# Two-layer cross-attention: where the turn of the row maxima stands in TensorE's order in layer 1

## The chip, the cores and the metric

One Trainium2 chip, of which the kernel uses one core. The metric is device microseconds (us) of one execution. The kernel before has three timed runs; their median is what a later time is held against.

## The reference, cut to what matters

Two layers of cross-attention follow each other, each with its own weights. There are 16 batches, 256 query rows of 320 channels, 20 heads of 16 channels, and 256 context rows of 512 channels, of which the first 252 are text and the last 4 are image tokens in layer 2; layer 1 takes the first 77 as text and the other 179 as image tokens. For layer 1:

```python
text = encoder_hidden_states[:, :77]
ip = encoder_hidden_states[:, 77:]
q = hidden_states @ Wq
probs = softmax(q_h @ k_h.T * scale)                 # per head, 77 text columns
text_probs = softmax(q @ k_text.T * scale)           # once over all channels
sem = (text_probs @ text) @ ip.T * scale
fused = q_h @ ip_k_h.T * scale + 0.5 * sem           # per head, 179 image columns
out = (probs @ v_h + spatial_mask * softmax(fused) @ ip_v_h) @ Wout + bout + hidden_states
```

Layer 2 is of the same kind, with a normalised semantic term. Each softmax subtracts a row maximum before its exp; this document is about where that maximum is brought into place in layer 1.

## The kernel before, in words

**Slots.** The work of layer 1 is cut into 80 slots, one for each batch and group of four heads (five groups a batch, so ten slots are two batches); layer 2 has 80 more. A slot of layer 1 takes some 7.7 us. `slot0(k)` (L783) writes down what TensorE does in slot k: the first half of the scores of slot k+2, the first half of the weights of slot k, attention on the values for slot k-1, the second half of the scores of k+2, the second half of the weights of k, the loads for slot k+4, and in the third quarter the turn of the maxima of k+2. Numbers between these steps (0.2, 0.6, 1.0) are places where `fill` puts in the work of other tasks that is due then: projections (L609, L612 queries with `hq` and outputs with `ho`; L239, L249 products of keys and values with weights `wA` to `wD`), transposes of `sp` (L685), scores for the semantic term (L666).

**The scores and their maxima.** `score0` (L737 on) writes four matmuls (L744) into the one score buffer `S`, which spans two banks. VectorE takes the maxima out of it in two reductions, L745 over the 77 text columns and L746 over the 179 others, into `mn`. Only then may the next half of scores go into `S`. So each slot has two score halves, each followed by its pair of reductions.

**The turn of the maxima.** `maxima0` (L748) is what the change moves. Two small matmuls (L752) with the identity turn `mn` of both halves into rows, in one of three `X` banks. ScalarE casts these rows to `mt` (L754, one buffer), and four DMAs of 2 KB each (L756), issued from ScalarE's own queue, put them into rows of the query stack `qs`. The second L752 needs the maxima of the second half, so it needs the L746 that follows the second L744 of the same slot.

**Who uses them.** `turned0` (L758 on) multiplies the key stack with the query stack, maxima rows included (L768, into two `T` banks); ScalarE takes the exp (L771), GpSimd multiplies by `rs` (L774). The second exp of slot k is ordered behind the last of the DMAs of the maxima of k+1. `attend0` multiplies with the values (L800, 24 matmuls into the single bank `P`), and `settle0` on VectorE transposes it (L811 into `nt`), takes the reciprocal (L814), multiplies (L815) and writes `tmp` (L817); L817 is the last to read bank `P`, so the next L800 waits for it. Every fifth slot the result of a batch is complete: `gather` (L830, transposes into `hT`) and `split` (L282 a cast on ScalarE; L283 and L284 on VectorE, into `ho`) prepare it for the output projection.

**What sets the order.** TensorE's order is what the program says. The order on ScalarE, VectorE, GpSimd and SyncE is set at build time by a scheduler that models a timeline, with a few instructions held in program order. So when TensorE's order changes, instructions on the other engines can change places too.

Of the kernel before, what the change touches and what calls it, by code (L numbers as in the profile page):

```python
# [38 lines left out]
SIZES = dict(RAW=2, KST=2, NP=4, NR=4, CTA=2, CTB=2, WB=4, M=2)  # L39
NS = B * NG  # L40
LEAD = 4


def RAMP(t):
# [6 lines left out]
def xattn2(  # L51
# [685 lines left out]
    def score0(k, t):  # L737
        Q, K = QK[k]
        if t == 0:
            maxes[k] = buf("mn", [128, 2, 4, 2], FR, bufs=2)  # L740
        mn = maxes[k]
        sp = scores(True)
        for h in range(4):
            mm(sp[:, h], Q[: XROW + T0, h, t * 128 : (t + 1) * 128], K[: XROW + T0, h], start=True, stop=True)  # L744
        nc.vector.tensor_reduce(mn[:, t, :, 0], sp[:, :, :T0], axis=AX.X, op=ALU.max)  # L745
        anchor(nc.vector.tensor_reduce(mn[:, t, :, 1], sp[:, :, T0:], axis=AX.X, op=ALU.max))  # L746
# [11 lines left out]
    def turned0(k, t):  # L758

        rs = get("s0", k // NG)[2]  # L760
        Q, K = QK[k]
        for p in range(2):
            if t == 0:
                P[k, p] = buf("P", [128, 2, 2, S], bufs=SIZES["NP"])
        st = [own("T").rearrange("p (h t) -> p h t", h=2) for p in range(2)]
        for p in range(2):
            for j in range(2):
                mm(st[p][:, j], K[:KS0, 2 * p + j, t * 128 : (t + 1) * 128], Q[:KS0, 2 * p + j], start=True, stop=True)  # L768
        for p in range(2):
            pt = P[k, p][:, t]  # L770
            exp = anchor(nc.scalar.activation(pt, st[p], AF.Exp, scale=SCALE))  # L771
            if t and k + 1 in issues:
                queued(exp, issues[k + 1])
            anchor(nc.gpsimd.tensor_mul(pt, pt, rs[:, t : t + 1].to_broadcast([128, 2, S])))  # L774

    def attend0(k):
        b, g = divmod(k, NG)
        v, pv = get("v0", b), own("P")
        for vt in range(3):
            values0(k, pv, v, vt)  # L780
        settle0(b, g, pv)

    def slot0(k):  # L783
        yield lambda: ahead(k + 2, 0)
        yield lambda: turned0(k, 0)
        yield 0.2
        if k > 0:
            yield lambda: attend0(k - 1)
        yield lambda: ahead(k + 2, 1)
        yield lambda: turned0(k, 1)  # L790
        yield lambda: stacks(k + LEAD)
        yield 0.6
        yield lambda: maxima(k + 2)
        yield 1.0

    def values0(k, pv, v, vt):
# [81 lines left out]
    def both1(k, t):  # L878

        a = k + 2 < 2 * NS and QK[k + 2]   # L880
        c = NS <= k < 2 * NS and QK[k]
        if a:
            if t == 0:
                maxes[k + 2] = buf("mn", [128, 4, 4], FR, bufs=2)[:, :2]
            sp = scores()
        def turned():
            for j in range(2):
                for u in range(2):
                    rows = slice(64 * u, 64 * u + KS1)
                    mm(st[u][:, j], c[1][rows, j, lo : lo + 128], c[0][rows, j], start=True, stop=True)  # L890

        def plain():
            for j in range(2):
                for u in range(2):
                    rows = slice(64 * u, 64 * u + XROW)
                    mm(sp[:, 2 * u + j], a[0][rows, j, t * 128 : (t + 1) * 128], a[1][rows, j], start=True, stop=True)  # L896
            image_scores(k + 2, t, sp)
            anchor(nc.vector.tensor_reduce(maxes[k + 2][:, t], sp[:, :, :T1], axis=AX.X, op=ALU.max))  # L898

        if c:  # L900
            st = [bank("T").rearrange("p (h t) -> p h t", h=2) for u in range(2)]
            lo = (0, DUP)[t]
        for wanted, make in ((a, plain), (c, turned))[:: 1 if t == 0 else -1]:
            if wanted:
                make()
        if c:
            for u in range(2):
                if t == 0:
                    P[k, u] = buf("P", [128, 2, 2, S], bufs=SIZES["NP"])
                anchor(nc.scalar.activation(P[k, u][:, t], st[u], AF.Exp, scale=SCALE))  # L910
# [13 lines left out]
    def rounded1(k, u):  # L924
        R[k, u] = buf("ctb", [128, 2, 2, S], FR, bufs=SIZES["CTB"], name="ph")
        W[k, u] = buf("wB", [128, 2, 2, S], bufs=SIZES["WB"], name="wt")
        for t in range(2):
            nc.scalar.activation(R[k, u][:, t], P[k, u][:, t], AF.Copy, scale=0.5)  # L928
            anchor(nc.gpsimd.tensor_sub(W[k, u][:, t], P[k, u][:, t], f(R[k, u][:, t])))  # L929
# [33 lines left out]
    def slot1(k):  # L963
# [12 lines left out]
        if mine:  # L976
            yield lambda: rounded1(k, 0)
        yield lambda: stacks(k + LEAD)
        if last:
# [207 lines left out]
    for c in range(B // 2):  # L1187
        n, k = 10 * c, [("k0", c)] if c else []
# [33 lines left out]
    def stacks(k):  # L1222
        if 0 <= k < 2 * NS:
            (stacks0 if k < NS else stacks1)(k)

    def ahead(k, t):
        if k < NS:
            score0(k, t)
        else:
            both1(k - 2, t)  # L1230

    def maxima(k):
        if k < 2 * NS:
            (maxima0 if k < NS else maxima1)(k)
# [225 lines left out]
```

## Time and profile before

| | |
|---|---|
| runs | 1503.99, 1501.08, 1503.84 us; median 1503.84 |
| profiled execution, its own time | 1502.55 us |
| its span in the trace | 1500.7 us |
| TensorE busy | 1422.2 us, 95% |
| VectorE busy | 1179.7 us, 79% |
| GpSimd busy | 1212.4 us, 81% |
| ScalarE busy | 889.5 us, 59% |
| TensorE's mean granted clock | 0.99 |

The trace covers the span; some 1.85 us of the execution's own time lie around it. Lines of instructions read: start in us, duration in us, engine, line of the kernel, operation, output<-inputs, how many in a row (x), and in brackets how long the engine stood idle before it and what it then waited for. Slots 28 to 38 of layer 1 lie from about 282 to 359 us, and layer 1 ends near 690 us.

### The profile page before, as it was taken

What the parts mean: (1) busy time and instruction counts of PE and PEld (TensorE: products, weight loads), DVE (VectorE), ACT (ScalarE), POOL (GpSimd) and SP (SyncE); (2) the same over time, 40 slices, a digit from 0 to 9 for tenths busy, and PEclk for the clock granted to TensorE, in tenths of its full rate; (3) what the DMA queues carried; (4) which work ended last, traced back from release to release, by engine and by line L of the source; (5) the groups of instructions that cost most, each with busy time, mean ns of one, the idle gap of its engine ahead of it and who ended that gap; (6) DMA issues with size and microseconds to landing.
All of it is one profiled execution on the core that took longest, in us unless ns stands there. A gap on an engine that the chain in (4) does not pass through costs nothing.

```text
span 1500.7 us, 36096 instructions
## 1 busy us (share of the span) xinstructions
PE 1422.2 (95%) x12740; PEld 1148.3 (77%) x12740; DVE 1179.7 (79%) x2593; ACT 889.5 (59%) x1975; POOL 1212.4 (81%) x1304
## 2 busy tenths in 40 slices
PE   8789999999999999789999999999999999999997
PEld 7678788888878877567777777777777777777765
DVE  5467777777778787878887788878877887788786
ACT  5356565656555655456665666566656665666563
POOL 4269797979787887898698779877987798779887
PEclk9799999999999999999999999999999999999999
DMA  7867777868676776774534434443444344433411
GB/s 234 202 200 211 199 221 196 226 190 223 185 207 193 219 217 167 199 214 145 165 99 130 124 116 118 131 128 112 121 131 128 110 122 127 130 109 99 121 30 44
DMA packets 230986, 234.32 MB, mean 156 GB/s; under 512 B 39127, under 2 KB 200678, under 8 KB 230790
## 3 DMA queue, kind: packets, MB, share of 16 engines
q1 hardware_dynamic: 228598, 230.71, 55.1%
q8 instruction: 102, 1.67, 0.5%
q10 hardware_dynamic: 2208, 1.30, 0.4%
q14 instruction: 78, 0.64, 0.1%
HBM read 118.04 MB, written 77.04 MB: 130 GB/s over the span
## 4 chain that ended last, share of the span: by engine, by line
PE 70%; DVE 13%; DMA 6%; POOL 5%; issue 3%; ACT 2%; SPq 1%; ACTq 0%; DVEq 0%; POOLq 0%
PE X L938 15%; PE X L239 14%; PE P L800 6%; PE X L609 5%; PE P L950 5%; PE P L960 4%; PE S L744 3%; PE T L890 3%; PE S L896 3%; DVE mn L746 3%; PE T L768 3%; PE X L612 2%; DVE nt L811 2%; PE X L578 2%; POOL P L774 1%
## 5 line engine op out<-in xcount | busy, mean ns | idle before, releaser
L774 POOL TENSOR_TENSOR P<-P,rs 128x512 f32<-128x512 f32 x320 | 413.7, 1314 | 89.8 <-ACT P L771 88.4
L929 POOL TENSOR_TENSOR wt<-P,ctb 128x512 f32<-128x512 f32 x320 | 410.7, 1307 | 74.0 <-ACT ctb L928 74.0
L938 PE MATMUL X<-ctb,gm 128*128 128x512 f32 x1120 | 305.4, 402 | 5.7 <-DVE wt L939 5.6
L771 ACT ACTIVATE P<-T 128x512 f32<-128x512 f32 x320 | 175.9, 595 | 151.1 <-PE T L768 120.6
L939 DVE TENSOR_TENSOR wt<-X,wt 128x512 f32<-128x512 f32 x320 | 216.5, 681 | 42.2 <-PE X L938 36.0
L938 PEld LDWEIGHTS X<-ctb,gm 128*128 128x128 f32 x1120 | 195.2, 188 | 39.0 <-DVE wt L939 8.6
L910 ACT ACTIVATE P<-T 128x512 f32<-128x512 f32 x320 | 173.2, 593 | 76.1 <-PE T L890 73.1
L928 ACT ACTIVATE ctb<-P 128x512 fp32r<-128x512 f32 x320 | 186.5, 627 | 38.9 <-PE X L938 33.5
L898 DVE TENSOR_REDUCE mn<-S 128x4 fp32r<-128x1008 f32 x160 | 191.5, 1197 | 0.0
L746 DVE TENSOR_REDUCE mn<-S 128x4 fp32r<-128x716 f32 x160 | 142.6, 891 | 0.0
L800 PE MATMUL P<-P,vr 128*32 128x256 f32 x1920 | 125.5, 392 | 7.2 <-DVE tmp L817 4.2
L744 PEld LDWEIGHTS S<-ks,qs 125*128 125x128 f32 x640 | 89.6, 194 | 39.9 <-issue 19.4
L744 PE MATMUL S<-ks,qs 125*128 125x256 f32 x640 | 114.4, 302 | 6.0 <-DMA ks<-M 3.7
L1027 POOL TENSOR_TENSOR r<-u,rs 128x40 f32<-128x40 f32 (+2 forms) x17 | 108.7, 6393 | 4.0 <-DVE u L1024 4.0
L745 DVE TENSOR_REDUCE mn<-S 128x4 fp32r<-128x308 f32 x160 | 74.9, 468 | 42.7 <-PE S L744 41.9
L768 PE MATMUL T<-qs,ks 127*128 127x256 f32 x640 | 105.5, 288 | 0.1
L800 PEld LDWEIGHTS P<-P,vr 128*32 128x32 f32 x1920 | 56.8, 112 | 48.2 <-issue 9.9
L768 PEld LDWEIGHTS T<-qs,ks 127*128 127x128 f32 x640 | 90.1, 194 | 0.9 <-issue 0.3
L950 PE MATMUL P<-P,v1t 128*32 128x256 f32 x1280 | 85.7, 385 | 0.0
L960 PE MATMUL P<-wt,zone 128*32 128x256 f32 x1280 | 84.6, 379 | 0.3 <-DVE wt L939 0.3
L811 DVE STREAM_TRANSPOSE nt<-P 128x512 f32<-128x512 f32 x80 | 57.0, 712 | 34.3 <-PE P L800 33.6
L239 PE MATMUL X<-wC,cta 128*128 128x324 f32 (+1 forms) x474 | 78.4, 312 | 0.0
(297 smaller groups left out, 2974.0 us busy)
## 6 DMA issues: line engine op xcount, KB each, us to landing
qd<-q SPq DMA_DIRECT2D x96, 256.0 KB
qs<-tph SPq DMA_DIRECT2D x64, 320.0 KB
rawc<-in_cT_dram SPq DMA_DIRECT2D x60, 256.0 KB
qs<-qd SPq DMA_DIRECT2D x80, 192.0 KB
ks<-kd SPq DMA_DIRECT2D x80, 192.0 KB
ks<-kd SPq DMA_DIRECT2D x160, 96.0 KB
qs<-qd SPq DMA_DIRECT2D x160, 96.0 KB
kd<-kst SPq DMA_DIRECT2D x57, 256.0 KB
```

What stands on the lines that cost most here:

```text
L239: last = mm(out, lhs(a, k), rhs(b, k), start=i == 0, stop=i == len(terms) - 1)
L744: mm(sp[:, h], Q[: XROW + T0, h, t * 128 : (t + 1) * 128], K[: XROW + T0, h], start=True, stop=True)
L746: anchor(nc.vector.tensor_reduce(mn[:, t, :, 1], sp[:, :, T0:], axis=AX.X, op=ALU.max))
L768: mm(st[p][:, j], K[:KS0, 2 * p + j, t * 128 : (t + 1) * 128], Q[:KS0, 2 * p + j], start=True, stop=True)
L771: exp = anchor(nc.scalar.activation(pt, st[p], AF.Exp, scale=SCALE))
L774: anchor(nc.gpsimd.tensor_mul(pt, pt, rs[:, t : t + 1].to_broadcast([128, 2, S])))
L800: mm(pv[32 * s : 32 * s + 32, o : o + S], v[:, vt, h : h + 32], P[k, s // 2][:, t, s % 2], start=vt < 2, stop=vt != 1,)
L898: anchor(nc.vector.tensor_reduce(maxes[k + 2][:, t], sp[:, :, :T1], axis=AX.X, op=ALU.max))
L928: nc.scalar.activation(R[k, u][:, t], P[k, u][:, t], AF.Copy, scale=0.5)
L929: anchor(nc.gpsimd.tensor_sub(W[k, u][:, t], P[k, u][:, t], f(R[k, u][:, t])))
L938: mm(yp, gm[:, gb], R[k, u][:, kt], start=i == 0, stop=i == len(blocks[n]) - 1)
L939: nc.vector.tensor_mul(W[k, u][:, n], yp, W[k, u][:, n])
```

## The change

The turn of the maxima of slot k+2 stood in the third quarter of slot k. It now stands at the very beginning of slot k+1, in front of that slot's first scores, for the maxima of slots 2 to 58. From slot 57 on the old place is kept, so slot 57 issues two turns, 58 at its start and 59 in its third quarter. Nothing is computed otherwise, and no instruction is added or taken away.

```diff
+SOON = 57
...
     def slot0(k):
+        if 0 < k <= SOON:
+            yield lambda: maxima(k + 1)
         yield lambda: ahead(k + 2, 0)
         yield lambda: turned0(k, 0)
         yield 0.2
...
         yield lambda: turned0(k, 1)
         yield lambda: stacks(k + LEAD)
         yield 0.6
-        yield lambda: maxima(k + 2)
+        if k >= SOON:
+            yield lambda: maxima(k + 2)
         yield 1.0
```

In the changed kernel line numbers are 1 higher up to the slot function and 4 higher behind it (the two L752 become L753, L744 to L746 become L745 to L747, L800 becomes L804, L811 L815, L817 L821, L830 L834; L283 and L284 become L284 and L285).

**TensorE, slot 32.** Before, the turn (L752) stands between two pieces of filling work, the products with `cta` and `ctb` alone and those with `wC`:

```order
L744 MATMUL S<-ks_101,qs_97 128x256 x4
L768 MATMUL T<-qs_95,ks_99 128x256 x4
L239 MATMUL X<-cta_81 77x192 x3
L239 MATMUL X<-cta_82 77x192 x3
L239 MATMUL X<-ctb_83 77x192 x3
L239 MATMUL X<-ctb_84 77x192 x3
L752 MATMUL X<-ident_r,mn_566 8x128 x2
L239 MATMUL X<-wC_92,cta_81 128x320 x3
L239 MATMUL X<-wC_92,cta_82 128x320 x3
L239 MATMUL X<-wC_92,ctb_83 128x320 x3
L239 MATMUL X<-wC_92,ctb_84 128x320 x3
L744 MATMUL S<-ks_102,qs_98 128x256 x4
```

Now the same piece of TensorE's order reads:

```order
L769 MATMUL T<-qs_95,ks_99 128x256 x4
L240 MATMUL X<-cta_81 77x192 x3
L240 MATMUL X<-cta_82 77x192 x3
L240 MATMUL X<-ctb_83 77x192 x3
L240 MATMUL X<-ctb_84 77x192 x3
L240 MATMUL X<-wC_92,cta_81 128x320 x3
L240 MATMUL X<-wC_92,cta_82 128x320 x3
L240 MATMUL X<-wC_92,ctb_83 128x320 x3
L240 MATMUL X<-wC_92,ctb_84 128x320 x3
L753 MATMUL X<-ident_r,mn_566 8x128 x2
L745 MATMUL S<-ks_102,qs_98 128x256 x4
```

The turn has moved behind the twelve `wC` matmuls and stands right in front of the next slot's first scores. On TensorE only these pairs move, 52 of the 80, each past 5 to 29 matmuls; the maxima of slots 10, 20, 30, 40 and 50 have no filling work in between and stay where they were.

**VectorE, slots 31 and 32 (place A in what follows).** The rows are the attention of slot 30 being settled (`nt_136`, `tmp_807`), with the gathering (`hT`) and splitting (`ho`) of a finished batch and the maxima of two slots (`mn_567` and `mn_566`). Before:

```order
L830 STREAM_TRANSPOSE hT_1308<-hsn 128x256
L167 TENSOR_TENSOR q_145<-X,q_145 128x256
L811 STREAM_TRANSPOSE nt_136<-P 128x512
L745 TENSOR_REDUCE mn_567<-S 128x4
L746 TENSOR_REDUCE mn_567<-S 128x4
L814 RECIPROCAL P<-nt_136 128x16
L283 TENSOR_TENSOR ho_161<-hT_1308,ho_161 128x512
L284 SCALAR_TENSOR_TENSOR ho_161<-ho_161,tmask,hT_1308 128x256
L815 TENSOR_TENSOR P<-P,mk 128x8
L260 TENSOR_TENSOR X<-X,kst_160 64x2x179
L817 TENSOR_TENSOR tmp_807<-nt_136,P 128x256
L745 TENSOR_REDUCE mn_566<-S 128x4
```

Now:

```order
L815 STREAM_TRANSPOSE nt_136<-P 128x512
L834 STREAM_TRANSPOSE hT_1300<-hsn 128x256
L746 TENSOR_REDUCE mn_567<-S 128x4
L747 TENSOR_REDUCE mn_567<-S 128x4
L818 RECIPROCAL P<-nt_136 128x16
L284 TENSOR_TENSOR ho_161<-hT_1300,ho_161 128x512
L285 SCALAR_TENSOR_TENSOR ho_161<-ho_161,tmask,hT_1300 128x256
L819 TENSOR_TENSOR P<-P,mk 128x8
L746 TENSOR_REDUCE mn_566<-S 128x4
L747 TENSOR_REDUCE mn_566<-S 128x4
L821 TENSOR_TENSOR tmp_807<-nt_136,P 128x256
L261 TENSOR_TENSOR X<-X,kst_160 64x2x179
```

The `hT` transpose has come to stand behind the attention's transpose, in front of the reductions, and the next pair of reductions has come in front of the multiplication that writes `tmp`. The same holds in slots 12, 22, 42 and 52.

**VectorE, slots 36 and 37 (place B).** Here `nt_135` is the attention of slot 35, `ho` the other batch, and the two pairs of reductions are those of the second half of slot 36 (`mn_566`) and of the first half of slot 37 (`mn_567`). Before:

```order
L830 STREAM_TRANSPOSE hT_1308<-hsn 128x256
L283 TENSOR_TENSOR ho_161<-hT_1308,ho_161 128x512
L284 SCALAR_TENSOR_TENSOR ho_161<-ho_161,tmask,hT_1308 128x256
L811 STREAM_TRANSPOSE nt_135<-P 128x512
L745 TENSOR_REDUCE mn_566<-S 128x4
L746 TENSOR_REDUCE mn_566<-S 128x4
L814 RECIPROCAL P<-nt_135 128x16
L815 TENSOR_TENSOR P<-P,mk 128x8
L817 TENSOR_TENSOR tmp_808<-nt_135,P 128x256
L745 TENSOR_REDUCE mn_567<-S 128x4
L746 TENSOR_REDUCE mn_567<-S 128x4
```

Now:

```order
L815 STREAM_TRANSPOSE nt_135<-P 128x512
L746 TENSOR_REDUCE mn_566<-S 128x4
L747 TENSOR_REDUCE mn_566<-S 128x4
L818 RECIPROCAL P<-nt_135 128x16
L834 STREAM_TRANSPOSE hT_1300<-hsn 128x256
L819 TENSOR_TENSOR P<-P,mk 128x8
L821 TENSOR_TENSOR tmp_808<-nt_135,P 128x256
L284 TENSOR_TENSOR ho_161<-hT_1300,ho_161 128x512
L285 SCALAR_TENSOR_TENSOR ho_161<-ho_161,tmask,hT_1300 128x256
L746 TENSOR_REDUCE mn_567<-S 128x4
L747 TENSOR_REDUCE mn_567<-S 128x4
```

The split into `ho` has moved from in front of the attention's transpose to behind `tmp`, right in front of the first half's reductions of slot 37. On ScalarE its cast (L282, now L283) now stands behind the cast of `rs` and two casts of `rawc` into `cta`, in front of which it stood. The same holds in slots 7, 17, 27, 47 and 57.

Elsewhere, near the end of the moved turns (**place C**, slots 57 to 59), VectorE's multiplication L455 of `rawc`, which needs a load, stands in front of the reductions of the second half of slot 57; before it stood behind them. On ScalarE the cast and the four DMA issues of a turn now stand around the two exps of the first half of a slot, where they were spread over a slot's end and the next one's beginning. GpSimd and SyncE have small moves only, and layer 2 keeps its order but for a few rows at the very end.

## The prediction

> **What bounds the kernel now.** I read the page first, then TensorE's waits and groups, then the timelines of the places where the order changes.
>
> ```profile
> PE 1422.2 (95%) x12740; PEld 1148.3 (77%) x12740; DVE 1179.7 (79%) x2593; ACT 889.5 (59%) x1975; POOL 1212.4 (81%) x1304
> ```
>
> TensorE is busy for 95% of the span, so only what shortens its waits, or adds to them, can move the time. TensorE's row of groups for the turn and its waits, first in slots 1 to 57 (75 to 521 us), then in the ten slots 28 to 37 (282 to 359 us), are:
>
> ```profile
> L752 PE MATMUL X<-ident_r,mn 128*8 128x128 f32 x160 | 30.4, 229 | 25.6 <-DVE mn L746 23.2 <-DVE mx L673 1.8
> ```
>
> ```profile
> PE X L752 <- DVE mn L746: 12.3, 22, 0.8
> PE P L800 <- DVE tmp L817: 2.3, 6, 0.4
> ...
> PE X L752 <- DVE mn L746: 2.3, 4, 0.8
> PE P L800 <- DVE tmp L817: 0.4, 1, 0.4
> ```
>
> The turn's wait for the reduction L746 is the largest wait of layer 1: 12.3 us in 22 places of slots 1 to 57, 2.3 us in every ten slots. The wait for L817 is the second, and it is the one that place A will touch. The 25.6 us of the whole group are not all in reach: 12.3 lie where turns are moved, the rest lie in the first 75 us and in slots 58 on, where nothing moves.
>
> **What goes.** TensorE's timeline, with a turn that doesn't wait, one that waits in full, and one that waits a little:
>
> ```profile
> 304.18 0.28 PE L752 MATMUL X<-ident_r,mn 128*8 128x128 f32 x2
> ...
> 318.65 0.22 PE L752 MATMUL X<-ident_r,mn 128*8 128x128 f32 x1
> 319.49 0.23 PE L752 MATMUL X<-ident_r,mn 128*8 128x128 f32 x1 [0.62 <-DVE mn L746]
> 319.56 1.09 PE L239 MATMUL X<-wC,cta 128*128 128x320 f32 x6
> 320.49 0.75 PE L239 MATMUL X<-wC,ctb 128*128 128x320 f32 x4
> ...
> 350.59 0.58 PE L752 MATMUL X<-ident_r,mn 128*8 128x128 f32 x2
> ```
>
> A pair that doesn't wait takes 0.28 us in all; the pair at 318.65 ends at 319.72, so it takes 1.07, or 0.79 more: the 0.62 of wait and some 0.16 of overlap that it loses. The pair at 350.59 takes 0.58, 0.30 more. So ten slots lose 2.3 + 4 x 0.16 + 0.30 = 3.24 us to the turn. In five times ten slots that is 16.2 us. The first slots have what is left of the 12.3 us, 12.3 - 5 x 2.3 = 0.8, and with two overlaps 1.1 us: **17.3 us in reach**.
>
> Would the wait really go? At the new place some filling work stands in front of the turn. For the turn above it is twelve `wC` matmuls, of which the two rows above cover ten in 1.7 us, against a wait of 0.79. A turn that comes that much later finds L746 done. What is late next is the first half of scores (L744) right behind it, which needs the same reduction to have emptied `S`; it comes after the same filling work, as before. So I take all 17.3 us away, on condition that VectorE does its reductions when it did.
>
> **What comes: place A, five times.** VectorE's and TensorE's timelines, slots 31 and 32:
>
> ```profile
> 308.29 0.43 DVE L830 STREAM_TRANSPOSE hT<-hsn 128x256 f32<-128x256 f32 x1
> 308.65 0.38 DVE L167 TENSOR_TENSOR q<-X,q 128x256 fp32r<-128x256 f32 x1
> 309.28 0.72 DVE L811 STREAM_TRANSPOSE nt<-P 128x512 f32<-128x512 f32 x1 [0.25 <-PE P L800]
> 309.93 0.48 DVE L745 TENSOR_REDUCE mn<-S 128x4 fp32r<-128x308 f32 x1
> 310.32 0.90 DVE L746 TENSOR_REDUCE mn<-S 128x4 fp32r<-128x716 f32 x1
> 311.13 0.25 DVE L814 RECIPROCAL P<-nt 128x16 f32<-128x16 f32 x1
> 311.29 1.39 DVE L283 TENSOR_TENSOR ho<-hT,ho 128x512 fp32r<-128x512 f32 x1
> 312.60 1.52 DVE L284 SCALAR_TENSOR_TENSOR ho<-ho,tmask,hT 128x256 fp32r<-128x256 f32 x1
> 314.11 0.52 DVE L260 TENSOR_TENSOR X<-X,kst 64x358 f32<-64x358 f32 x1
> 314.55 0.40 DVE L817 TENSOR_TENSOR tmp<-nt,P 128x256 f32<-128x256 f32 x1
> ```
>
> ```profile
> 315.10 1.50 PE L800 MATMUL P<-P,vr 128*32 128x256 f32 x24 [0.43 <-DVE tmp L817]
> ```
>
> The attention matmuls already wait here for L817, so every delay of L817 shows in full. L830 (308.29 to the next start at 308.65, 0.36) moves behind L811 into this chain, a pair of reductions (309.93 to 311.22, 1.29) comes in front of L817, and L260 (314.11 to 314.55, 0.44) leaves it: 0.36 + 1.29 - 0.44 = **1.2 us**. The lower bound is given by the other L284 below, which takes 0.47 in place of 1.52: then 0.2. The upper: on ScalarE three DMA issues of the turn now stand in front of the cast that feeds L283,
>
> ```profile
> L756 ACTq DMA_DIRECT2D qs<-mt x312: 569/570/1203, 64.2 to 682.7; - x156
> ```
>
> and one of them at its longest instead of its median adds 0.63: 1.8 us. The median issues end just before VectorE is ready for `ho`, so I take 1.2, five times: 6.0 us.
>
> **Place B, six times.** ScalarE's, VectorE's and TensorE's timelines, slots 36 and 37:
>
> ```profile
> 346.39 0.82 ACT L282 CAST ho<-hT 128x768 fp32r<-128x768 f32 x1
> ...
> 349.82 1.15 ACT L164 CAST cta<-rawc 128x512 fp32r<-128x512 f32 x2
> ```
>
> ```profile
> 347.25 1.45 DVE L283 TENSOR_TENSOR ho<-hT,ho 128x512 fp32r<-128x512 f32 x1 [1.12 <-ACT ho L282]
> 348.62 0.47 DVE L284 SCALAR_TENSOR_TENSOR ho<-ho,tmask,hT 128x256 fp32r<-128x256 f32 x1
> ```
>
> ```profile
> 355.43 0.74 PE L744 MATMUL S<-ks,qs 125*128 125x256 f32 x4
> ```
>
> The cast of `ho` now follows the two `cta` casts, so it runs from 350.97 to 351.79. L283 (1.45) ends at 353.24, L284 at 353.7 to 354.8 (0.47 or 1.52), and the pair of reductions behind them (1.29) at 355.0 to 356.1. TensorE comes for `S` at 355.43: it waits 0 to 0.6 us, up to 1.0 if the cast is held up as well. I take 0.5, six times: 3.0 us.
>
> Which of the two L284 values holds depends on GpSimd:
>
> ```profile
> 309.47 4.37 POOL L774 TENSOR_TENSOR P<-P,rs 128x512 f32<-128x512 f32 x3
> ...
> 348.81 0.23 POOL L434 MEMSET M<- 77x154 f32 x1 [0.67 <-PE X L696]
> ```
>
> The slow L284 (312.60) lies wholly beside a GpSimd multiplication, the fast one (348.62) beside 0.2 us of GpSimd idle and a MEMSET. GpSimd works at both places of the changed kernel unless its multiplications come later, so I took the slow one for A. The Trainium skill, page "GPSIMD Engine Reference", section "1. Specifications", says that GpSimd shares its memory interfaces with VectorE, with contention where a VectorE instruction has two inputs there; these rows agree, and by it A falls to 0.2 wherever GpSimd is idle beside L284, which would make the sum 5 us better.
>
> **Place C, once.** SyncE's, VectorE's and TensorE's timelines, slots 57 to 59:
>
> ```profile
> 518.98 0.52 SPq L84 DMA_DIRECT2D rawc<-in_cip_dram  x1
> ```
>
> ```profile
> 521.53 1.04 DVE L455 TENSOR_TENSOR rawc<-rawc 64x512 f32<-64x512 f32 x1 [0.37 <-DMA rawc<-in_cip_dram]
> ...
> 522.57 1.43 DVE L284 SCALAR_TENSOR_TENSOR hq<-hq,tmask,xq 128x256 fp32r<-128x256 f32 x1
> ```
>
> ```profile
> 521.60 0.29 PE L752 MATMUL X<-ident_r,mn 128*8 128x128 f32 x2
> ...
> 525.13 1.24 PE L800 MATMUL P<-P,vr 128*32 128x256 f32 x17
> ...
> 529.19 0.23 PE L752 MATMUL X<-ident_r,mn 128*8 128x128 f32 x1 [1.22 <-DVE mn L746]
> ```
>
> With L455 in front, the reductions of slot 57 start at 522.57 and end at 523.86, and the turn that ran at 521.60 waits 2.3 us. L817, now behind L284 and another pair of reductions, moves from before 525.13 to about 529, some 1.6 us beyond that. Behind it the turn at 529.19 loses the 1.22 of wait that it had, but runs at about 532.5. Net **3.3 us**; 0 if the load comes with the earlier stream and is there in time, 5 if both stalls add up. Another 0.3 us comes in slot 4, where L817 also gets two instructions in front.
>
> A stall of 2.3 us could also cost clock. Two windows (their length, then the busy time of TensorE, its weight loads, VectorE, ScalarE and GpSimd, then granted clock, share of the DMA engines and GB/s), and TensorE's longest waits from 600 to 650 us:
>
> ```profile
> 515.00:690.00 175.00, 154.72 (x1434) 125.65 (x1432) 142.37 (x315) 94.54 (x222) 146.80 (x164) 0.96 0.71 194
> ...
> 600.00:650.00 50.00, 39.18 (x361) 30.36 (x365) 42.73 (x94) 25.42 (x60) 42.59 (x45) 0.90 0.75 199
> ```
>
> ```profile
> PE X L752 <- DVE mx L673: 1.8, 1, 1.8
> ```
>
> No wait there was over 1.8 us, and yet the granted clock fell to 0.90, a loss of at most 5 us of TensorE's time. The Trainium skill, page "TensorE: Matmul & The Clock Gate", section "HAM oscillation — how this bites in real kernels", has the rule that TensorE should have no idle gap over some 3.4 us; by it C costs no clock. This trace speaks against relying on that. I leave the clock out of the sum and put it into the slower case.
>
> **The sum.** -17.3 + 6.0 + 3.0 + 0.3 + 3.3 = -4.7 us against the profiled execution's own 1502.55 (span 1500.7 and 1.85 around it): 1497.9. The median of the runs, 1503.84, is 1.3 above that execution, so the forecast is **1499.1** as a median. A measurement of this kernel can tell about 0.2%, 3 us, from no change; the forecast is just beyond that.
>
> **The rivals.**
> 1. *The whole gain.* VectorE has room (79% busy), ran ahead in the changed places, and A, B and C cost nothing: 1503.84 - 17.3 = 1486.5. For it: the lower bounds of A, B and C are all near 0. Against it: L800 waits for L817 at place A already. Chance 0.17.
> 2. *The wait only moves.* The first scores behind the turn need the same reduction; where VectorE's pair comes later, TensorE waits at L744 in place of L752, or the lead of layer 1 is given back from 521 us on, where loads set the pace. 1503.8. For it: from 515 to 690 us TensorE is idle for 20 of 175 us, so there is room to lose it. Against it: the filling work in front is longer than the wait. Chance 0.18.
> 3. *Slower: VectorE's queue.* Long instructions (the `ho` pair, L455) stand in front of L817 and the reductions, and TensorE stalls there for longer than the turn did. It decides once 5 A + 6 B + 0.3 + C exceeds 17.3. At the upper bounds 5 x 1.8 + 6 x 1.0 + 0.3 + 5 = 20.3, or +3.0, and with 0 to 5 us of lost clock, 1506.8 to 1511.8; I take 1508.5. For it: every upper bound has a row. Against it: all must come together. Chance 0.20.
>
> **How the numbers follow.** The forecast has a chance of 0.45, with its own range 1494 to 1503, from the bounds of A and B at less than their ends together: a fifth of it, 0.09, lies above 1500.8, within 3 us of no change. Faster: 0.17 + 0.36 = 0.53. Same: 0.18 + 0.09 = 0.27. Slower: 0.20. The range leaves out the lower half of the whole gain and the upper half of the slower case: 1488 to 1508. So faster is likely by a little more than even, and a gain of a few us is the likeliest.
>
> **What would show it.** Right: in slots 1 to 57 the turn's wait for the reduction falls from 12.3 us to under 2; at the end of place A L800's wait for the L817 of before grows from 0.43 to about 1.6, once in ten slots; the second scores at B wait about 0.5 for their reduction; the load of `rawc` is named on VectorE just ahead of the reductions at C. Wrong: the turn, or the scores behind it, still waits for the reduction in every ten slots; new waits for the maxima's DMAs ahead of L768; ten slots of 77 us that shrink by over 2.5 or not at all; or a stretch after 521 us that grows by as much as layer 1 gained.

## The result, and the profile after

The changed kernel takes **1499.46 us** (median of 22 runs, 1495.32 to 1511.36), the kernel before 1504.20 (22 runs, 1501.08 to 1508.17): a ratio of 0.997, interval 0.9956 to 0.9983. That is 4.7 us faster, and 0.36 us from the forecast. Its profiled execution took 1499.52 us with a span of 1497.7, 3.0 below the execution profiled before.

The size came out as forecast, but several terms did not. First TensorE's group of the turn:

```profile
L753 PE MATMUL X<-ident_r,mn 128*8 128x128 f32 x160 | 25.6, 225 | 16.6 <-DVE mn L747 14.5 <-DVE mx L674 2.1
```

TensorE's waits, first in slots 1 to 57 (75 to 521 us), then in ten slots (282 to 359 us):

```profile
PE X L610 <- ACT mt L755: 4.0, 5, 0.8
PE X L753 <- DVE mn L747: 2.8, 2, 1.7
PE X L667 <- DVE q L262: 1.5, 3, 0.8
...
PE X L610 <- ACT mt L755: 0.8, 1, 0.8
PE X L240 <- DVE sp L670: 0.6, 1, 0.6
```

The turn's wait fell from 12.3 us in 22 places to 2.8 in two, and those two are new (slot 4 and place C). In ten slots the 2.3 us are gone, and so is the 0.4 for L817. A wait of 0.8 for an `X` bank has come, once in ten slots.

Where the time went is best seen from the starts of the attention matmuls (L800, now L804), the first of the 24 for each slot's values, in the two traces, and in that of the best experiment below:

| values of slot | before, us | changed | lead of the changed kernel | best experiment (slots 4 to 54) | its lead |
|---|---|---|---|---|---|
| 2 | 92.33 | 92.25 | 0.1 | 90.95 | 1.4 |
| 4 | 106.75 | 110.92 | -4.2 | 105.46 | 1.3 |
| 5 | 114.99 | 118.37 | -3.4 | 112.92 | 2.1 |
| 55 | 501.51 | 492.80 | 8.7 | 486.80 | 14.7 |
| 56 | 509.62 | 500.64 | 9.0 | 494.91 | 14.7 |
| 58 | 525.13 | 519.64 | 5.5 | 510.40 | 14.7 |
| 79 | 695.61 | 691.22 | 4.4 | 681.48 | 14.1 |
| end of the span | 1500.7 | 1497.7 | 3.0 | 1485.4 | 15.3 |

So the changed kernel loses 4.2 us in slots 3 and 4 and has 0.8 of it back by slot 5, gains 12.1 us over fifty slots (5 to 55), 2.4 in every ten, and loses 3.5 between slots 56 and 58, 1.1 in the rest of layer 1, and 2.6 at the very end, before which layer 2 had given 1.2. The trace names causes for the losses in slots 3 and 4, at place C and at the end.

**Slots 3 and 4.** VectorE's operation on the weight `wF`, before and in the changed kernel (there with the second reduction behind it):

```profile
95.90 1.34 DVE L167 TENSOR_TENSOR wF<-rawc,wF 128x256 fp32r<-128x256 f32 x1
```

```profile
95.18 0.42 DVE L168 TENSOR_TENSOR wF<-rawc,wF 128x256 fp32r<-128x256 f32 x1 [2.02 <-ACT wF L165]
...
96.53 0.88 DVE L747 TENSOR_REDUCE mn<-S 128x4 fp32r<-128x716 f32 x1
```

ScalarE's and its queue's timeline, then TensorE's, in the changed kernel:

```profile
94.69 0.46 ACT L165 CAST wF<-rawc 128x320 fp32r<-128x320 f32 x1 [1.29 <-DMA rawc<-in_wo_dram]
94.69 1.97 ACTq L757 DMA_DIRECT2D qs<-mt  x3
96.77 1.08 ACT L772 ACTIVATE P<-T 128x512 f32<-128x512 f32 x2 [1.62 <-DMA qs<-mt]
```

```profile
97.46 0.23 PE L753 MATMUL X<-ident_r,mn 128*8 128x128 f32 x1 [1.19 <-DVE mn L747]
...
98.88 1.36 PE L769 MATMUL T<-qs,ks 127*128 127x256 f32 x3 [0.37 <-DMA qs<-mt]
100.17 2.79 PE L804 MATMUL P<-P,vr 128*32 128x256 f32 x24
```

ScalarE's cast of the weight (L165) waits for its load, and two queues stand behind it. On VectorE, L168 needs that cast and now stands in front of the pair of reductions; before, it stood behind them and waited for nothing. So the reductions end at 97.41 instead of 95.83, and the turn waits 1.19 us for them. On ScalarE, three DMA issues of the turn and both exps stand behind the cast, and the products of key and query stack (L769) wait 0.37 us for a DMA of the turn. Then TensorE's attention matmuls take 2.79 us instead of 1.50. The window from 95 to 105 us, before and after, shows why:

```profile
95.00:105.00 10.00, 9.20 (x84) 8.03 (x84) 8.01 (x23) 5.97 (x17) 9.39 (x10) 1.00 0.61 149
```

```profile
95.00:105.00 10.00, 8.42 (x54) 5.69 (x54) 7.69 (x20) 4.08 (x13) 6.29 (x7) 0.68 0.39 97
```

The granted clock fell from 1.00 to 0.68.

**Place C.** VectorE's and TensorE's timelines of the changed kernel:

```profile
513.43 1.25 DVE L456 TENSOR_TENSOR rawc<-rawc 64x512 f32<-64x512 f32 x1 [1.45 <-DMA rawc<-in_cip_dram]
514.61 0.46 DVE L746 TENSOR_REDUCE mn<-S 128x4 fp32r<-128x308 f32 x1
514.99 0.88 DVE L747 TENSOR_REDUCE mn<-S 128x4 fp32r<-128x716 f32 x1
```

```profile
515.93 0.23 PE L753 MATMUL X<-ident_r,mn 128*8 128x128 f32 x1 [1.65 <-DVE mn L747]
```

As forecast, VectorE waits for the load of `rawc` in front of the reductions, and the turn waits 1.65 us for them. That is not the whole loss: 1.4 of the 3.5 us are gone by the attention of slot 57 (509.59 against 517.14), before that load, with a wait of 0.81 us for `q`:

```profile
508.76 0.90 PE L667 MATMUL X<-kb,q 128*128 128x156 f32 x6 [0.81 <-DVE q L262]
```

L262 now stands behind a pair of reductions in VectorE's queue; before, L261 stood in front of them.

**The end of layer 2.** One row of ScalarE and one of TensorE before, the two timelines in the changed kernel, and the last 27 us as windows, before and after:

```profile
1482.54 0.48 ACT L1091 CAST hq<-X 128x384 fp32r<-128x384 f32 x1 [7.43 <-PE X L1088]
```

```profile
1483.07 1.32 PE L1097 MATMUL X<-wF,hq 128*128 128x320 f32 x5
```

```profile
1477.08 0.83 ACT L283 CAST ho<-hT 128x768 fp32r<-128x768 f32 x1 [7.54 <-DVE hT L1074]
1477.82 0.47 ACT L1095 CAST hq<-X 128x384 fp32r<-128x384 f32 x1
```

```profile
1478.35 0.41 PE L1101 MATMUL X<-wF,hq 128*128 128x320 f32 x1 [0.73 <-ACT hq L1095]
1479.42 0.86 PE L1101 MATMUL X<-wF,hq 128*128 128x320 f32 x4 [0.67 <-DVE hq L1096]
...
1480.82 1.72 PE L964 MATMUL P<-wt,zone 128*32 128x256 f32 x16
```

```profile
1470.00:1497.00 27.00, 21.53 (x160) 15.81 (x148) 18.69 (x46) 6.65 (x13) 21.25 (x28) 1.00 0.10 30
```

```profile
1470.00:1497.00 27.00, 17.67 (x112) 13.20 (x102) 15.24 (x39) 2.89 (x6) 15.00 (x22) 0.90 0.14 42
```

Here the casts of `ho` and `hq` have changed places: `hq`, for which TensorE waits, now comes second. TensorE waits 0.73 and 0.67 us where it waited for neither, and the clock falls again: 3.4 us of the window, from 1481.1 us on, run at half clock; the rest of the fall to 0.90 lies behind TensorE's last matmul. The rows of order that move here lie over 950 us behind the last turn that moves.

### The profile page after: what moved, and what is told of

It is laid out like the page before. It is cut to its first block, busy times and chain, and to the rows that moved or that the text cites. A ratio compares the mean times of both kernels' runs of the same rounds, so it can differ in the third digit from the quotient of the medians.

```text
span 1497.7 us, 36123 instructions
## 1 busy us (share of the span) xinstructions
PE 1427.8 (95%) x12740; PEld 1155.6 (77%) x12740; DVE 1170.2 (78%) x2593; ACT 884.8 (59%) x1975; POOL 1215.2 (81%) x1304
## 4 chain that ended last, share of the span: by engine, by line
PE 73%; DVE 8%; DMA 6%; POOL 6%; issue 3%; ACT 3%; SPq 1%; ACTq 0%; DVEq 0%; POOLq 0%
PE X L942 15%; PE X L240 14%; PE P L804 6%; PE X L610 5%; PE P L954 5%; PE S L745 5%; PE P L964 4%; PE T L769 4%; PE T L894 3%; PE S L900 3%; PE X L613 2%; PE X L250 2%; PE X L579 2%; POOL P L775 2%; DVE mn L747 1%
## 5 line engine op out<-in xcount | busy, mean ns | idle before, releaser
L747 DVE TENSOR_REDUCE mn<-S 128x4 fp32r<-128x716 f32 x160 | 142.2, 889 | 0.0
L804 PE MATMUL P<-P,vr 128*32 128x256 f32 x1920 | 127.4, 396 | 5.3 <-DVE tmp L821 2.0
L745 PE MATMUL S<-ks,qs 125*128 125x256 f32 x640 | 117.7, 307 | 4.9 <-DMA ks<-M 2.8
L745 PEld LDWEIGHTS S<-ks,qs 125*128 125x128 f32 x640 | 89.0, 195 | 40.1 <-issue 20.9
L769 PE MATMUL T<-qs,ks 127*128 127x256 f32 x640 | 108.2, 292 | 0.4 <-DMA qs<-mt 0.4
L746 DVE TENSOR_REDUCE mn<-S 128x4 fp32r<-128x308 f32 x160 | 74.4, 465 | 31.2 <-PE S L745 30.8
L815 DVE STREAM_TRANSPOSE nt<-P 128x512 f32<-128x512 f32 x80 | 56.9, 711 | 51.8 <-PE P L804 51.3
L769 PEld LDWEIGHTS T<-qs,ks 127*128 127x128 f32 x640 | 92.1, 198 | 2.0 <-DMA qs<-mt 1.0
L804 PEld LDWEIGHTS P<-P,vr 128*32 128x32 f32 x1920 | 57.2, 112 | 47.0 <-issue 8.1
L610 PE MATMUL X<-ho,wF 128*128 128x256 f32 x512 | 74.3, 287 | 6.5 <-ACT mt L755 4.0
```

Source lines behind the costliest of these rows:

```text
L804: mm(pv[32 * s : 32 * s + 32, o : o + S], v[:, vt, h : h + 32], P[k, s // 2][:, t, s % 2], start=vt < 2, stop=vt != 1,)
```

## The experiments

Times are medians, with the ratio to the kernel before on the same chip and its interval.

### Turns from slot 5 on

```diff
-SOON = 57
+SOON, FROM = 57, 5
...
-        if 0 < k <= SOON:
+        if FROM <= k <= SOON:
...
-        if k >= SOON:
+        if k >= SOON or k + 1 < FROM:
```

> Turns move only from slot 5 on (maxima of 6 to 58), so the turns of slots 2 to 5 keep their old place. Theory (the change loses some 3.5 to 4 us in slots 3 and 4, because its DMA issues stand behind a cast that waits for a weight load, and TensorE's stall there halves the clock): the loss goes and the two or three small waits of those slots come back, 0.3 us; about 3.5 us faster than the changed kernel, 1496. In the trace slot 5 starts no later than before, and the granted clock from 95 to 105 us is 1.00. Rival (the clock's phase near the beginning falls anyhow, and the loss is chance): 1499.5, as the changed kernel, with a half-clock stretch elsewhere in the first 120 us.

Measured: 1501.43 us, 0.997 (0.995 to 0.999), runs from 1492.14 to 1507.11. The loss in slots 3 and 4 did go: the attention of slot 4 starts at 106.60 (before 106.75, changed 110.92), so it comes from the turns there. But the time did not fall, and its runs spread over 15 us. Three jumps of 2.5 to 3.9 us at slots 8, 18 and 38 stand in the trace (of the slowest of the twelve runs), which neither theory had. VectorE's, GpSimd's and TensorE's timelines at slot 18:

```profile
211.93 3.42 DVE L285 SCALAR_TENSOR_TENSOR hq<-hq,tmask,xq 128x256 fp32r<-128x256 f32 x1 [0.16 <-ACT hq L283]
```

```profile
208.43 5.00 POOL L775 TENSOR_TENSOR P<-P,rs 128x512 f32<-128x512 f32 x4
213.40 1.25 POOL L284 TENSOR_TENSOR hq<-xq,hq 128x512 fp32r<-128x512 f32 x1
214.61 0.44 POOL L822 TENSOR_TENSOR hsn<-tmp 128x128 f32<-128x128 f32 x1
```

```profile
215.54 2.17 PE L240 MATMUL X<-cta,wB 128*128 128x360 f32 x6 [2.47 <-DVE sp L670]
```

An operation that takes some 0.5 us by itself takes 3.42 and ends at 215.35, 0.30 us after GpSimd's unbroken run has ended at 215.05. VectorE's queue stands behind it, and TensorE waits 2.47 us; its next matmuls run at a lower clock (0.83 from 212 to 222 us). This gave a new theory, which the other traces bear out only in part: **VectorE's operation with two inputs in SBUF is held until GpSimd pauses**, and whether it meets such a run is decided by small shifts.

### Turns up to slot 54

```diff
-SOON = 57
+SOON = 54
```

> Turns move up to slot 54 only (maxima of 2 to 55), by which the multiplication of rawc stands behind the reductions of slot 57 as before. Theory (place C costs 3.3 us): 3.3 us come back, three turns fewer lose about 0.8 of gain; 2.5 us faster than the changed kernel, 1497. In the trace the lead at slot 60 is about 8 us, not 6.4. Rival (from 521 us on loads set the pace, and any lead over 6 us is given back there): 1499.5, the lead at slot 68 again 6 us.

Measured: 1498.86 us, 0.9981 (0.996 to 1.0002). The lead over before is 10.0 us at slot 56 and 10.0 at slot 58 (515.08 against 525.13): the loss at C is gone, and 7.6 us of the lead are left at slot 79. So C's price was C's, the wait for `q` in slot 57 included. The median did not fall as forecast, 4.4 us below the kernel before where the changed kernel was 4.7 below; in this profile slots 3, 4 and 8 lost 5.4 us, the last by a held `hq`.

### Turns from slot 4 to slot 55

```diff
-SOON = 57
+SOON, FROM = 55, 4
...
-        if 0 < k <= SOON:
+        if FROM <= k <= SOON:
...
-        if k >= SOON:
+        if k >= SOON or k + 1 < FROM:
```

> Turns move from slot 4 to slot 55 (maxima of 5 to 56). Slot 4's cast has no DMA issues of the turn around it, place C keeps the order of before, and at the end of layer 2 the cast of hq stands in front of that of ho, as before. Theory (three local losses of 3.5 to 4, 3.3 and 2.6 us that add up): some 8.5 us faster than the changed kernel, 1491, 13 below the kernel before. Rival (the losses are not local, time saved in one place is waited out in the next): 1496 or above.

Measured: **1492.61 us, 0.993 (0.9907 to 0.9952)**. The losses add up as local ones: 10.6 us faster than before. The lead grows from 1.2 us at slot 5 to 14.3 at slot 55. Slot 58 still lost 4.0 us: TensorE waits 2.52 us there for a small VectorE operation that stands in its queue behind the multiplication of `rawc`, which waits for its load, and `hq`.

### Without every tenth turn

```diff
+WHICH = lambda k: k % 10 != 3
...
+    def early(k):
+        return 2 <= k <= SOON + 1 and WHICH(k)
...
-        if 0 < k <= SOON:
+        if early(k + 1):
...
-        if k >= SOON:
+        if not early(k + 2):
             yield lambda: maxima(k + 2)
```

> As the changed kernel, but each tenth turn, 3, 13, 23 and so on to 53, which did not wait before, keeps its old place. In the changed kernel the output projection at place A waits 0.8 us for the X bank that this turn holds until its cast. Theory (that wait is the price of A): it goes, five times 0.8, and the time falls by some 4 us, to 1495.5; L804 then waits for L821 at most as before, 0.4. Rival (the price of A is the late L817, as predicted, and was only hidden behind the bank): the wait comes back at the attention matmuls, 0.8 to 1.2 in each ten slots, and the time stays at 1499.5.

Measured: 1501.02 us, 0.9988 (0.997 to 1.0006): the time says no, the trace says why. Up to slot 36 the lead is 10.8 us, against 3.4 in the changed kernel (343.19 and 350.61 against 354.00). Of these 7.4 us, 4.8 are there by slot 8, since slot 4 lost nothing in this execution; the other 2.6 come at the three places A between, 0.9 at each. There TensorE waits neither for the bank nor for L825 (the L817 of before), so the wait did not come back as the rival had it. Then 7.1 us are lost at once, at place B. VectorE's, GpSimd's and TensorE's timelines:

```profile
341.23 5.88 DVE L285 TENSOR_TENSOR ho<-hT,ho 128x512 fp32r<-128x512 f32 x1 [1.36 <-ACT ho L284]
```

```profile
341.18 1.29 POOL L169 TENSOR_TENSOR cta<-rawc,cta 128x512 fp32r<-128x512 f32 x1
342.43 0.45 POOL L826 TENSOR_TENSOR hsn<-tmp 128x128 f32<-128x128 f32 x1
342.85 1.28 POOL L169 TENSOR_TENSOR cta<-rawc,cta 128x512 fp32r<-128x512 f32 x1
344.07 2.49 POOL L776 TENSOR_TENSOR P<-P,rs 128x512 f32<-128x512 f32 x2
```

```profile
348.76 1.22 PE L746 MATMUL S<-ks,qs 125*128 125x256 f32 x4 [4.07 <-DVE mn L748]
```

GpSimd runs from 341.18 to 346.56 without a pause, and `ho` ends at 347.11. The reductions stand behind it, and the second scores wait 4.07 us, at place B as forecast but at eight times its price; then the granted clock is 0.57 from 347 to 355 us.

### Turns from slot 4 to slot 54

The edit is that of the third experiment, with `SOON, FROM = 54, 4`.

> Turns move from slot 4 to slot 54 (maxima of 5 to 55). As the kernel with slots 4 to 55, but with one turn fewer, by which TensorE comes to slot 58 as the kernel with turns up to slot 54 did, which lost nothing there; the kernel up to 55 lost 4 us in that slot. Theory (the loss at slot 58 hangs on where the turns of 56 and 57 stand): some 3 us faster than the kernel with slots 4 to 55, 1490. Rival (the load of rawc lands at its own time, so that the lead is eaten there whatever the turns do): 1492.6, as that kernel.

Measured: **1488.95 us, 0.9914 (0.9888 to 0.994)**, the best of all, 15 us faster than before. Nothing is lost at slot 58 (the table above). The only turn that stands elsewhere than in the kernel with slots 4 to 55 is that of the maxima of 56, so the loss did hang on it, and not on the load alone. The other traces agree: the four kernels that move turns in slot 55 or later lose 2.0 to 4.0 us between the attention of slots 57 and 58, the seven that stop at slot 54 or earlier 0.6 or less.

### The third operation of hq on GpSimd

On top of the kernel with slots 4 to 54:

```diff
-        order(nc.vector.scalar_tensor_tensor(hl[:, 2], f(hl[:, 2]), neg, src[:, 2], op0=ALU.mult, op1=ALU.add))
+        if tag == "hq":
+            order(nc.gpsimd.tensor_sub(hl[64:, 2], src[64:, 2], f(hl[64:, 2])))
+        else:
+            order(nc.vector.scalar_tensor_tensor(hl[:, 2], f(hl[:, 2]), neg, src[:, 2], op0=ALU.mult, op1=ALU.add))
```

> As the kernel with turns moved from slot 4 to slot 54, and the third operation of hq (two inputs in SBUF) goes from VectorE to GpSimd, as a subtraction on the 64 partitions where it does anything; the result is the same. In the traces so far this operation took 0.5 to 1.5 us on VectorE, but 3.4 to 3.7 in four places where GpSimd multiplied without a pause, and TensorE lost 2.5 to 3.9 us in each of those slots. Theory (VectorE is held while GpSimd runs on, and whether it hits is chance): no operation on VectorE for hq over 2 us, the runs spread less, and the median is 1 to 3 us below the kernel without this. Rival (the stretches are the sign of something else, a load that is late): the losses stay, and GpSimd's 0.6 us more for each of 32 batches makes it 0 to 5 us slower.

Measured: 1549.4 us, 1.0326 (1.028 to 1.0372), far slower than either theory had it. The held `hq` is gone, but `ho` at place B is now held in every ten slots. The operation's rows, TensorE's waits (90 to 520 us), and one case on GpSimd:

```profile
L284 DVE TENSOR_TENSOR ho<-hT,ho x32: 673/1478/6307, 118.0 to 1531.3; 128x512 fp32r<-128x512 f32 x32
```

```profile
PE S L748 <- DVE mn L750: 22.3, 5, 4.5
```

```profile
204.42 2.47 POOL L778 TENSOR_TENSOR P<-P,rs 128x512 f32<-128x512 f32 x2
```

In that case `ho` starts at 201.17, takes 6.28 us, and ends 0.56 us after GpSimd's last multiplication (206.89). Five such cases cost TensorE 22.3 us of waits and some 30 us of its lead, in jumps of 4.0 to 7.5 at slots 7, 17, 27, 37 and 47. Some 12 us more than in the kernel with slots 4 to 54 are lost at the five places A, and another 11 in layer 2, which the edit also touches. It is the strongest evidence for the hold, in a place where I had not looked for it.

### Only the turns that waited, and only the others

```diff
-SOON = 57
+EARLY = [k for k in range(5, 55) if k % 10 in (1, 4, 5, 7, 8)]
...
-        if 0 < k <= SOON:
+        if k + 1 in EARLY:
...
-        if k >= SOON:
+        if k + 2 not in EARLY:
```

The second has `k % 10 in (0, 2, 3, 6, 9)`.

> Of the turns 5 to 54 only those move that waited for their reduction before: 1, 4, 5, 7 and 8 of each ten. Theory (the gain is those waits, and nothing else): the same gain as all turns from 5 to 55 give, 1490 to 1492.6, or up to 4 us more, since turn 3 of each ten no longer holds an X bank. Rival (the gain comes from the whole run of turns standing later, which gives ScalarE and VectorE room): half of it, 1497.

> Of the turns 5 to 54 only those move that did not wait before: 2, 3, 6 and 9 of each ten. Theory (the gain is the waits of the others): none, 1503.2, and up to 4 us slower by the bank that turn 3 holds. Rival (a gain from the later place itself): half of it, 1497.

Measured: the waiting turns alone 1491.55 us, 0.992 (0.9898 to 0.9943); the others alone 1504.6, 1.0009 (0.9992 to 1.0025). TensorE's wait at the turn from 75 to 500 us, in the first and the second:

```profile
PE X L753 <- DVE mn L747: 0.8, 2, 0.6
```

```profile
PE X L753 <- DVE mn L747: 13.9, 23, 0.9
```

The theory holds from both sides, as far as the medians tell: the five turns of ten that waited give 12.9 us, where all turns from slot 4 to 54 gave 15.5, and the others alone give nothing.

### Without turn 3, and without 3 and 7, in slots 5 to 54

The same edit with `k % 10 != 3`, and with `k % 10 not in (3, 7)`.

> The turns 5 to 54 move but for 3 of each ten, which did not wait before and whose X bank the output projection at place A waits for by 0.8 us. Theory (prices that add): as the kernel with turns 5 to 55, whose slots 4, 58 and the end lose nothing, less five times 0.8: 4 us below it, 1485. Rival (the bank's wait is replaced by that for L821, with which the attention matmuls come on the heels): 1489, no change.

> As the kernel before this one, and turn 7 of each ten keeps its old place too, with its wait of 0.79 us; by that VectorE's order at place B is that of the kernel before, with the split into ho in front of the attention's transpose. Theory (B costs 0.1 to 0.7 us in each ten slots, and some runs more, where VectorE's ho is held beside GpSimd): the two prices about cancel, 1485 to 1488, and the profile shows no operation of ho over 2 us in slots 37, 47 and so on. Rival (B's order costs nothing, as its profile in the changed kernel would have it): 4 us slower than the kernel before this one, 1489.

Measured: without turn 3 1491.07 us, 0.9912 (0.9891 to 0.9933), runs from 1484.19 to 1494.84; without 3 and 7 1494.99, 0.9943 (0.9928 to 0.9959), runs from 1494.06 to 1496.39. The bank's wait (75 to 500 us) in the kernel with slots 4 to 54, and without turn 3:

```profile
PE X L610 <- ACT mt L755: 4.1, 5, 0.8
```

```profile
PE X L613 <- ACT mt L755: 0.2, 1, 0.2
```

The bank's wait goes as the theory said, and no wait for L821 comes in its place. The median did not fall to 1485, only the fastest run did: in the profiled run, the slowest of the six, `hq` was held for 3.68 and 3.44 us, at 133.11 and 285.40; what kept the others above 1485 no trace shows. With turn 7 back at its old place the time rises by 3.9. The turn's wait comes back (from 75 to 500 us 3.9 us in seven places, against 0.8 in two), but waits for L821 (2.9 in six, against 0.8 in one) and of L667 for `q` (4.2 in five, against 0.3 in two) come too. So this speaks for the rival, that B's order costs next to nothing where nothing is held, but does not show it. The six runs lie within 2.3 us, and no operation in the profile is held.

## Why the prediction was right, and where it was not

**The signs.** Of the four signs of being right only the load of `rawc` was seen as written. The turn's wait fell to 2.8 us, not under 2; the attention's wait at place A did not grow but went; the second scores at B wait some 0.1 us, not 0.5. Ten slots shrank by 2.4 us, just short of the 2.5 named as a sign of being wrong. So the time is nearer to the forecast than the working behind it.

**What bounds the kernel, and what goes: right.** 17.3 us were put in reach. The turn's 22 waits are gone, none moved to the scores behind it, and the two experiments that split the turns put the gain on those that waited.

**Place A: wrong term.** 1.2 us at the attention matmuls were forecast, through a late L817; their wait is gone instead. VectorE's, GpSimd's and TensorE's timelines in the changed kernel:

```profile
310.07 0.67 DVE L284 TENSOR_TENSOR ho<-hT,ho 128x512 fp32r<-128x512 f32 x1
310.66 1.52 DVE L285 SCALAR_TENSOR_TENSOR ho<-ho,tmask,hT 128x256 fp32r<-128x256 f32 x1
...
313.38 0.40 DVE L821 TENSOR_TENSOR tmp<-nt,P 128x256 f32<-128x256 f32 x1
```

```profile
310.26 3.05 POOL L775 TENSOR_TENSOR P<-P,rs 128x512 f32<-128x512 f32 x2 [1.01 <-ACT P L772]
```

```profile
312.70 1.21 PE L610 MATMUL X<-ho,wF 128*128 128x256 f32 x8 [0.81 <-ACT mt L755]
313.92 1.50 PE L804 MATMUL P<-P,vr 128*32 128x256 f32 x24
```

The first `ho` operation began in a pause of GpSimd (309.25 to 310.26) and took 0.67, not 1.39, so L821 ends at 313.78, in time. The price came 1.2 us earlier, as a wait for an `X` bank: the turn right ahead of the slot holds it until ScalarE's cast at 312.29. That this wait does not merely hide one for L821 is shown by the kernels without turn 3 in which all other turns move: there TensorE waits for neither at place A. The step that failed weighed the turn's matmuls and not the bank that they take.

**Place B: right place, wrong bounds.** 0.5 us forecast, from 0 to 1.0. In the changed kernel's profile it is about 0.1, in an experiment 4.07, in another 4.5 five times over. The upper bound was worked out from an operation that had met GpSimd for a moment (1.52), as if that were the longest it could take. The runs show that it can be held until an unbroken run of GpSimd ends. It need not be: in the changed kernel eleven such operations at places A and B (five L285, six L284) all got in between two GpSimd operations of a run that went on, as L285 at A above (310.66 to 312.18, the run until 313.31). So did this `hq`, beside five GpSimd operations in a row from 209.99 on:

```profile
213.25 0.81 DVE L285 SCALAR_TENSOR_TENSOR hq<-hq,tmask,xq 128x256 fp32r<-128x256 f32 x1
```

```profile
209.99 5.22 POOL L775 TENSOR_TENSOR P<-P,rs 128x512 f32<-128x512 f32 x4
215.17 1.28 POOL L284 TENSOR_TENSOR hq<-xq,hq 128x512 fp32r<-128x512 f32 x1
```

In all twelve traces 14 of some 1200 operations that write `ho` or `hq` took over 2 us, one of them in the kernel before. The Trainium skill, "GPSIMD Engine Reference", section "1. Specifications", names the contention for two inputs; that section does not say how long it can last, and here it was up to 5.6 us. Slot 37 also costs 0.7 us that the prediction does not have (8.18 us from the attention of slot 36 to that of slot 37, before 7.50), at L613 and L667. The kernel without turns 3 and 7, with B's old order, loses there too (8.47, with a wait of 0.84 for `q`), so this is not the price of the moved `ho`.

**Slot 4: wrong.** 0.3 us were forecast, 4.2 came. The step counted what had come to stand in front of L817, not in front of the reductions: an operation that waits for a cast that waits for a load, the mechanism of place C. On ScalarE the turn's DMA issues and two exps had come to stand behind the same cast, and the lower clock added the rest; the experiments do not part the three. The loss is no fixed price: the kernel without every tenth turn has the same order on both engines there, its VectorE waits 0.67 us for the cast instead of 2.02, and it lost nothing (its attention of slot 4 starts at 106.07), so it hangs on when the load lands.

**Place C: right mechanism, size in part by luck.** 3.3 forecast, 3.5 measured. The mechanism named accounts for 2.1 of it: the turn waits 1.65 us, not 2.3, the attention behind the late L817 waits 0.33, not some 1.6, and the turn behind it still waits 0.90 (before 1.22). The other 1.4 came with the wait for `q`, which the prediction did not have.

**The end of layer 2: not seen.** A swap of two casts there costs 1.4 us of waits and some more by the clock, 2.6 us in all by the lead (5.6 at the last products, 3.0 at the end).

**Ten slots**: -1.5 forecast (-3.2 + 1.2 + 0.5), -2.4 measured. With A and B together some 0.9 too dear in each ten, and slot 4 and the end 6.5 too cheap, the errors largely cancelled. The forecast owes its nearness to that, which is luck.

**The clock.** Half-clock stretches followed TensorE waits of 1.19 and 0.37 us (95 to 105 us, 0.68) and of 0.73 and 0.67 (the end, 0.90). Yet at place C waits of 0.81, 1.65, 0.33 and 0.90 us within 15 us left the granted clock at 1.00 (505 to 530 us), so C cost no clock. What decides is not shown. The rule of the Trainium skill, "TensorE: Matmul & The Clock Gate", section "HAM oscillation — how this bites in real kernels", is to leave no idle gap over some 3.4 us. The prediction doubted that shorter gaps cost no clock, and the first two places bear it out, with no wait over 1.7 us near them.

**What stays open.** Why an operation is held in one run and gets in at once in another is not known: an `hq` that began 3.26 us into a row of four GpSimd multiplications took 0.81 us in the changed kernel (at 213.25), and one that began 3.25 us into such a row took 3.68 in the kernel without turn 3 (at 133.11, the row from 129.86). That the wide spread of the changed kernel's runs (16 us, before 7) comes from such holds was argued from the profiles of single executions, not shown for each run.

## What to carry to other kernels

Move an instruction past work that is longer than its wait, only where it waits, and then read the order of every other engine around the place, above all for operations that wait for a load, and ScalarE's DMA issues too: here five turns in ten carried the gain, and a few places at the edges gave some two thirds of it back. A VectorE operation with two SBUF inputs in front of something that TensorE needs should have the longest unbroken run of GpSimd beside it as its upper bound, even where its usual time is far shorter.

## What the hardware showed that was not expected

An operation on VectorE with two inputs in SBUF that meets an unbroken run of GpSimd can fare in two ways. Mostly it gets in between two GpSimd operations (L285 at place A, 1.52 us). Sometimes it makes no visible progress until the run ends: `ho` takes 0.67 us when it starts in a pause; in the cases above it ended 0.55 and 0.56 us after GpSimd's run, and `hq` 0.30 us after it, whether it had waited 2 or 5 us. The other surprise is the clock: in two places it fell behind two waits of TensorE of 0.4 to 1.2 us within 2 us of each other, and in a third a wait of 1.65 us left it as it was.
